# Turning activations by DMA transpositions of 16-bit planes instead of TensorE transpositions, in a transformer stack on one core

## The chip, the core and the metric

The kernel runs on one core of one Trainium2 chip. The metric is the device time of one execution in microseconds (us). TensorE (PE, with its weight loads PEld) multiplies and transposes into PSUM; VectorE (DVE), ScalarE (ACT) and GpSimd (POOL) work on SBUF, the first two on PSUM as well; SyncE (SP) issues all DMAs here. Every engine works through its own queue in order and waits for others by semaphores.

## The reference, cut to what matters

The input has 8 sequences of 1024 rows of 256 numbers, all in 32-bit floats. Four blocks follow one another, each with a residual around it:

```
x = x + decoder_layer(layernorm(x))     # linear attention with 16 heads and cumulative sums along the
                                        #   rows, then x @ Wo, layernorm, gelu MLP 256-1024-256, layernorm
x = x + relu(layernorm(x) @ w1 + b1) @ w2 + b2                 # MLP 256-1024-256
x = x + softmax(q k^T / 16) v,   q, k, v from layernorm(x)     # attention over the 1024 rows
x = x + fp4(silu(g) * u) @ fp4(w_down)^T                       # g, u = fp4(layernorm(x)) @ fp4(w_gate / w_up)^T
```

fp4() rounds each 16 numbers of a row to a 4-bit grid with their own scale. Every product contracts over the columns of its left operand, so rows of activations must be turned (columns onto the partitions) before TensorE can take them.

## The kernel before

A chunk is 128 rows, a group 4 chunks; a sequence has two groups, and there are 16 groups. The parts of the program are Python generators: linear attention by groups (`linear_group`, `linear_span`, `linear_chunk`), the two MLPs (`dense`, with `norms_1` and `norms_2` after each), and softmax attention with the fp4 MLP by chunks (`soft_chunk`). A generator yields what it needs next: the engine, the tiles that must be ready, PSUM banks or a fresh buffer, and a due time `at`. The class `Plan` keeps an estimated clock of every engine and of every tile, takes the part whose need is met first on TensorE's clock, and writes its instructions down; each engine's order is then fixed by dependencies (`Queue.issue`). Where the plan foresees TensorE pausing for more than 1.6 us, `fill` puts in dummy products of the identity for the pause less 0.7 us. Nearly all instructions are recorded at one line, L342.

Buffers of each kind come from fixed sets (`TILES`); late in the kernel `SPARE` lets prob tiles lie in flow's buffers, soft in lin's, rows in x's, and the tiles of q and k serve as two more `hid`. The weights of the MLPs are streamed through four buffers each (`w_in`, `w_out`): their loads wait on SP until TensorE has used the buffer.

Rows are turned in two ways:

- `turned` transposes 128x128 pieces on TensorE against the identity into a PSUM bank, and ACT (or DVE, for every second probT) copies the bank to SBUF. It serves n0T (two pieces a chunk), k (two), probT (eight), xqT (two) and hqT (six).
- `flip` serves h, n and n2T, three pairs of pieces a chunk. POOL copies the 32-bit rows into two planes of 16-bit halves (`cut`), SP issues one DMA transposition of the four 128x128 planes (`spun`), and ACT interleaves the halves again into the target.

Of the kernel before, what the change touches and what calls it, by code (L numbers as in the profile page):

```python
# [9 lines left out]
F32 = mybir.dt.float32  # L10
I32 = mybir.dt.int32
BF16 = mybir.dt.bfloat16
U16 = mybir.dt.uint16
# [4 lines left out]
P = 128  # L18
# [26 lines left out]
    "x": (4, D, F32),  # L45
    "n0": (2, D, F32),
    "lin": (4, D, F32),
    "flow": (9, 512, F32),
    "xr": (2, D, F32),
    "norm": (3, D, F32),  # L50
    "hidden": (LAG + 2, D, F32),
    "soft": (5, D, F32),
    "prob": (7, 512, F32),
    "rows": (4, D, F32),
    "hid": (3, INTER_PAD, F32),
    "q_c": (2, INTER, BF16),
    "cut": (2, 2 * D, U16),
    "spun": (2, 2 * D, U16),
}


# [4 lines left out]
class Plan:  # L66
# [96 lines left out]
    def took(self, queue, op, args, kw):  # L163

        aps = [x for x in list(args) + list(kw.values()) if isinstance(x, bass.AP)]
        outs = [kw["out"] if "out" in kw else aps[0]]
        if kw.get("accum_out") is not None:
            outs.append(kw["accum_out"])
        size = 1
        for ap in aps:  # L170
            n = 1
            for d in ap.shape[1:]:
                n *= d
            size = max(size, n)

        overlap, after = 0.0, 0.035
        if queue == "tensor":
            size = 1
            for d in outs[0].shape[1:]:
                size *= d  # L180
            cost = size * (0.853e-3 if op == "transpose" else 1.687e-3)
            tiled = op == "matmul" and (kw["lhsT"].shape[-1] <= 32 or kw["lhsT"].shape[0] <= 32)
            if tiled or op == "matmul" and kw["lhsT"].dtype == BF16:
                cost *= 0.25
            if tiled != self.tiled:
                cost += 0.2
            self.tiled = tiled
            after = 0.2
        elif queue == "vector":
            each = {"reciprocal": 6.2e-3, "tensor_tensor_scan": 2.15e-3}.get(op, 1.05e-3)  # L190
            cost = 0.17 + each * size
            if op == "tensor_scalar" and outs[0].dtype == BF16:
                cost = 0.16 + 0.26e-3 * size
            elif op == "scalar_tensor_tensor" and any(ap.shape[-1] == 1 for ap in aps):
                cost += 0.06
            overlap = 0.08
        elif queue == "scalar":
            cost = (0.16 if op == "copy" else 0.26) + 0.82e-3 * size
            for x in args:
                if not isinstance(x, bass.AP) and self.SETS.get(x, self.act_set) != self.act_set:  # L200
                    self.act_set = self.SETS[x]
                    self.free[queue] = self.free.get(queue, 0.0) + 1.3
            if kw.get("accum_out") is not None:
                cost += 0.15
            overlap = 0.1
        elif queue == "gpsimd":
            cost = 0.65 + 0.7e-3 * size
            if op in ("tensor_scalar", "iota"):
                cost = 0.22
            elif op == "memset":  # L210
                cost = 0.1 + 0.9e-3 * size
            elif op == "tensor_copy":
                cost = 0.15 + 1.0e-3 * size
        else:
            cost = 0.4
        start = self.free.get(queue, 0.0)
        if queue not in ("tensor", "sync"):
            start = max([start] + [self.used.get(ap.tensor.name, 0.0) for ap in outs])
        for ap in aps:
            name = ap.tensor.name  # L220
            if self.by.get(name) != queue or queue in ("vector", "gpsimd"):
                start = max(start, self.done.get(name, 0.0) + (0.05 if queue == "gpsimd" else 0.0))
            if name not in self.done and name in self.held:
                start = max(start, self.used[name])
        if queue == "tensor":
            if start - self.ran > 2.0:
                self.slow = start + 2.1
            if start < self.slow:
                cost *= 2
            self.ran = start + cost  # L230
        if queue == "sync":
            start = max(start, self.landed.pop(0))
        end = start + cost
        if queue == "sync":
            n = 2e-6 / 150e-3 if op == "dma_start_transpose" else 4e-6 / 250e-3
            for d in outs[0].shape:
                n *= d
            self.free["rings"] = max(self.free.get("rings", 0.0), end) + n
            after = self.free["rings"] - end + 2.1
            self.landed.append(end + after)  # L240
        self.free[queue] = end - overlap
        for ap in outs:
            self.done[ap.tensor.name] = end + after
            self.by[ap.tensor.name] = queue
        for ap in aps:
            name = ap.tensor.name
            self.used[name] = max(self.used.get(name, 0.0), end + after)
            if queue != "tensor" and name not in self.kept:
                self.held.discard(name)
# [111 lines left out]
def block_stack_kernel(ctx: ExitStack, tc: tile.TileContext, a: dict, out: bass.AP):  # L361
# [272 lines left out]
            nc.tensor.transpose(bank[:, i, :], src, ident)  # L634
        return bank[:, : len(srcs), :]

    def flip(src, dst):

        cut = yield from fresh("cut", plan.pool(src))
        nc.gpsimd.tensor_copy(  # L640
            cut.rearrange("p (h f) -> p h f", h=2),
            src.bitcast(U16).rearrange("p (f h) -> p h f", h=2),
        )
        plan.drop(src)
        spun = yield from fresh("spun", dma(cut))
        nc.sync.dma_start_transpose(out=spun.rearrange("p (b t) -> p b t", t=P), in_=cut)
        plan.drop(cut)
        yield act(spun)
        nc.scalar.copy(
            dst.bitcast(U16).rearrange("p k (t h) -> p k t h", h=2),  # L650
            spun.rearrange("p (h k t) -> p k t h", h=2, t=P),
        )
        plan.drop(spun)

    def table(func):

# [265 lines left out]
    def turn_half(p, kind, i, src):  # L922
        dst = half_of(p, kind, i // 2)
        j = i % 2
        yield from flip(src, dst[:, :, j * P : (j + 1) * P])
        n = groups[p]["turned"]
        n[kind, i // 2] = n.get((kind, i // 2), 0) + 1

    def linear_group(p):
# [9 lines left out]
        def front(i):  # L939
# [4 lines left out]
            rc = groups[p]["res"][i] = kept([P, D], "res", RES)  # L944
            n0 = yield from layernorm("n0", x)
            plan.drop(x)
            yield pe(n0, banks=1)
            bank = turned(halves(n0))
            yield act(bank)
            nc.scalar.copy(n0T[:, :, i * P : (i + 1) * P], bank)  # L950
            fronts.add(i)
            yield plan.need("gpsimd", (n0, bo), when=lambda: "norm" in late)
            nc.gpsimd.tensor_tensor(rc, n0, bo, ALU.add)
# [193 lines left out]
    def linear_chunk(p, i, n0T, comp, qk):  # L1147
# [86 lines left out]
            scores.append(sc)  # L1234
        end = g == NG - 1 and i == G - 1
        if not end:
            yield pe(banks=1, at=at + 0.66 + 0.06 * i, when=lambda: count["attended"] == c)
            bank = turned([qk[1][:, k, here] for k in range(2)])
            kT = two((yield from fresh("lin", act(bank), "k")))
            nc.scalar.copy(kT, bank)  # L1240
        kv = past.get("kv")
        yield pe(
            pad,
# [237 lines left out]
    def norms_2(p, i, acc, taken):  # L1481
# [15 lines left out]
            q["n2T"][g] = two(kept([P, 2 * GT], "n2T", 4))  # L1497
        n2 = q["n2T"][g]
        here = slice(i * P, (i + 1) * P)
        yield from flip(n, n2[:, :, here])  # L1500
        yield pe(
            n2,
            banks=1,
# [14 lines left out]
    def soft_chunk(cc):  # L1518
# [49 lines left out]
            plan.let_go(banks[kb])  # L1568
        rows = yield from fresh("rows", dma())
        nc.sync.dma_start(out=rows, in_=q["rows", c])  # L1570
        probT = []
        for kb in range(NG):
            yield pe(prob[kb], banks=1, at=at + 0.25)
            bank = turned([prob[kb][:, j * P : (j + 1) * P] for j in range(G)])
            plan.drop(prob[kb])
            tp = yield from fresh("prob", act(bank) if kb % 2 else dve(bank), "probT")
            tp = tp.rearrange("p (k t) -> p k t", k=G)
            (nc.scalar.copy if kb % 2 else nc.vector.tensor_copy)(tp, bank)
            probT.append(tp)
        yield pe(*probT, banks=1)  # L1580
        rsum = small([P, 1], "rsum")
        nc.vector.tensor_reduce(rsum, sums, AX.X, ALU.add)
        nc.vector.reciprocal(rsum, rsum)
# [14 lines left out]
        n = yield from layernorm("soft", rows)  # L1598
        yield dve(n)
        yield from fp4(n, D)  # L1600
        yield pe(n, banks=1, at=at + 0.5, when=lambda: "fp4" in weights)
        bank = turned(halves(n))
        plan.drop(n)
        xqT = two((yield from fresh("soft", act(bank), "xqT")))
        nc.scalar.copy(xqT, bank)
        hid = None
        for j0 in range(0, INTER, INTER // 2):
            cols = slice(j0, j0 + INTER // 2)
            yield pe(xqT, banks=2)
            gb, ub = mm_bank()[:, : INTER // 2], mm_bank()[:, : INTER // 2]  # L1610
            for bank, wT in ((gb, wgT), (ub, wuT)):
                for k in range(2):
# [14 lines left out]
        plan.drop(xqT)  # L1627
        yield dve(hid)
        yield from fp4(hid, INTER)
        hqT = []  # L1630
        for half in range(2):
            yield pe(hid, banks=1, at=at + 0.75)
            tiles = INTER_TILES[4 * half : 4 * half + 4]
            bank = turned([hid[:, f0 : f0 + P] for f0, _ in tiles])
            hqT.append((yield from fresh("prob", act(bank), "hqT")))
            hqT[half] = hqT[half].rearrange("p (k t) -> p k t", k=4)
            nc.scalar.copy(hqT[half][:, : len(tiles), :], bank)
        yield pe(*hqT, banks=1)
        bank = mm_bank()
        for k in range(len(INTER_TILES)):  # L1640
            nc.tensor.matmul(
# [3 lines left out]
                start=k == 0,  # L1645
                stop=k == len(INTER_TILES) - 1,
            )
        plan.drop(hid, *hqT)
        count["out"] += 1
        y = yield from fresh("soft", dve(bank), "y")  # L1650
        nc.vector.tensor_tensor(y, bank[:, :D], rows, ALU.add)
# [68 lines left out]
```

## Time and profile before

| | before |
|---|---|
| three runs, us | 2618.31, 2614.11, 2616.58 (median 2616.58) |
| profiled execution, us | 2618.8, span 2617.1 |
| granted TensorE clock | 0.997 |
| TensorE busy in the span | 98% |
| VectorE, ScalarE, GpSimd busy | 74%, 51%, 27% |
| DMA queue 1, share of 16 engines | 33.1% |
| DMA transpositions | 192 |

Times in rows of the profile are microseconds, means of one instruction nanoseconds. A group's row has the engine, the operation, the tiles written and read by the program's names, the shapes and the count; then the busy time, the mean of one, and the engine's idle time just before with what ended it. Spans of matmuls overlap since they are pipelined: their steps from start to start are read from the timeline. A product of 32-bit floats appears as two records, a transposition as one. L342 is the helper that records every instruction, so groups are told apart by tiles.

### The profile page before, as it was taken

How to read it: one execution, taken by the hardware profiler on the slowest of the kernel's cores; microseconds unless marked ns; L12 is line 12 of the kernel's file. 1: busy time of each engine (PE TensorE's matmuls, PEld its weight loads, DVE VectorE, ACT ScalarE, POOL GpSimd, SP SyncE). 2: the span in 40 equal slices, each digit the busy share in tenths (PEclk: the TensorE clock that was granted, in tenths of full speed). 3: DMA queues.
4: the chain of work that ended last, by engine and by line, in shares of the span. 5: the costliest groups of instructions: out<-in, count | busy, mean ns of one | idle time of the engine just before them, and what ended most of it. 6: DMA issues, size and time to landing. Idle time of an engine off the chain costs nothing.

```text
span 2617.1 us, 46326 instructions
## 1 busy us (share of the span) xinstructions
PE 2571.5 (98%) x16593; PEld 2010.4 (77%) x16593; DVE 1947.3 (74%) x4352; ACT 1344.0 (51%) x2658; POOL 703.0 (27%) x1293
## 2 busy tenths in 40 slices
PE   8998999999999999999999999999999999999999
PEld 7777777877777777777877877777777777878777
DVE  6788796867769587685868768677785877855687
ACT  3535636464475544645555464645545545454443
POOL 2343332332313232131321322313231231311000
PEclk9999999999999999999999999999999999999999
DMA  2445443333323342322433323333333423333100
GB/s 75 125 121 154 115 117 95 109 88 107 86 80 101 85 115 68 108 80 85 117 81 92 97 75 99 92 108 81 99 82 83 115 72 96 88 87 89 31 5 21
DMA packets 391268, 237.11 MB, mean 91 GB/s; under 512 B 129152, under 2 KB 379520, under 8 KB 391040
## 3 DMA queue, kind: packets, MB, share of 16 engines
q1 hardware_dynamic: 391040, 234.16, 33.1%
q8 instruction: 132, 2.16, 0.4%
q14 instruction: 96, 0.79, 0.1%
HBM read 188.17 MB, written 20.71 MB: 80 GB/s over the span
## 4 chain that ended last, share of the span: by engine, by line
PE 80%; DVE 13%; ACT 3%; DMA 1%; issue 1%; POOL 1%; SPq 0%; DVEq 0%; POOLq 0%; ACTq 0%
PE bank L342 80%; DVE hid L342 2%; DVE prod L342 2%; DVE n L342 1%; ACT L342 1%; DVE ln_st L342 1%; DVE u L342 1%; DVE res L342 1%; DVE ln_mv L342 0%; DVE x_amax L342 0%; DMA spread<-packed 0%; DVE div L342 0%; DVE spread L342 0%; DVE mx L342 0%; DMA spun<-cut 0%
## 5 line engine op out<-in xcount | busy, mean ns | idle before, releaser
L342 PE MATMUL bank<-half,w_in 128*128 128x256 f32 x2048 | 533.4, 384 | 7.3 <-DVE v L342 4.5
L342 PE MATMUL bank<-w_out,hidden 128*128 128x256 f32 x2048 | 529.4, 383 | 2.7 <-DMA w_out<-in_L_ffn_w_dram 1.6
L342 POOL TENSOR_SCALAR ln_ve<-ln_mv 128x1 f32<-128x1 f32 x384 | 96.9, 252 | 1607.8 <-DVE ln_mv L342 1591.3
L342 PEld LDWEIGHTS bank<-w_out,hidden 128*128 128x128 f32 x2048 | 374.0, 190 | 105.2 <-issue 53.2
L342 PEld LDWEIGHTS bank<-half,w_in 128*128 128x128 f32 x2048 | 384.3, 191 | 85.6 <-issue 22.5
L342 ACT ACT_TABLE_LOAD x321 | 411.8, 1283 | 17.3 <-DVE nmax L342 11.6
L342 ACT ACTIVATE hidden<-bank,c_L_ffn_b 128x256 f32<-128x256 f32 x256 | 120.6, 472 | 269.4 <-PE bank L342 269.1
L342 POOL TENSOR_TENSOR ln_rstd<-ln_ve,neghalf 128x1 f32<-128x1 f32 x384 | 236.3, 615 | 32.0
L342 PE MATMUL bank<-n2T,qT 128*128 128x512 f32 x512 | 241.6, 594 | 0.4 <-ACT qT L342 0.2
L342 PE MATMUL bank<-vt,probT 128*128 128x256 f32 x1024 | 232.0, 380 | 0.0
L342 PEld LDWEIGHTS bank<-vt,probT 128*128 128x128 f32 x1024 | 193.1, 190 | 30.2 <-issue 3.0
L342 ACT ACTIVATE hidden<-bank,c_L_attn_b 128x256 f32<-128x256 f32 x256 | 119.7, 468 | 183.3 <-PE bank L342 182.8
L342 PE MATMUL bank<-wdT,hqT 128*128 128x256 f32 x768 | 176.6, 380 | 1.2 <-ACT hqT L342 1.0
L342 PE MATMUL bank<-wgT,xqT 128*128 128x352 f32 x512 | 173.8, 462 | 0.0
L342 PE MATMUL bank<-wuT,xqT 128*128 128x352 f32 x512 | 172.4, 459 | 0.0
L342 ACT COPY half<-spun 128x512 uint16<-128x512 uint16 x128 | 86.3, 674 | 150.1 <-DMA spun<-cut 149.6
L342 PEld LDWEIGHTS bank<-wdT,hqT 128*128 128x128 f32 x768 | 145.3, 190 | 22.7 <-ACT hqT L342 1.4
L342 DVE TENSOR_TENSOR sc<-bank,triu 128x512 f32<-128x512 f32 x240 | 149.7, 680 | 8.5 <-PE bank L342 8.0
L342 PEld LDWEIGHTS bank<-n2T,qT 128*128 128x128 f32 x512 | 93.4, 190 | 69.1 <-issue 60.5
L342 PEld LDWEIGHTS bank<-wuT,xqT 128*128 128x128 f32 x512 | 97.4, 190 | 54.1
L342 DVE TENSOR_TENSOR hid<-hid,bank 128x352 f32<-128x352 f32 x116 | 59.7, 515 | 101.4 <-PE bank L342 79.2
L342 PEld LDWEIGHTS bank<-wgT,xqT 128*128 128x128 f32 x512 | 93.7, 190 | 37.1 <-issue 4.3
(220 smaller groups left out, 4530.2 us busy)
## 6 DMA issues: line engine op xcount, KB each, us to landing
w_in<-in_L_attn_W_dram SPq DMA_DIRECT2D x256, 128.0 KB
w_out<-in_L_attn_W_dram SPq DMA_DIRECT2D x256, 128.0 KB
w_in<-in_L_ffn_w_dram SPq DMA_DIRECT2D x256, 128.0 KB
w_out<-in_L_ffn_w_dram SPq DMA_DIRECT2D x256, 128.0 KB
spread<-packed SPq DMA_DIRECT2D x90, 256.0 KB
x<-in_L_attn_inputs_dram SPq DMA_DIRECT2D x64, 128.0 KB
xr<-in_L_attn_inputs_dram SPq DMA_DIRECT2D x64, 128.0 KB
rows<-res SPq DMA_DIRECT2D x64, 128.0 KB
```

Of the source, the lines that this page charges most:

```text
L342: ins = method(*args, **kw)
```

## The change

All rows that `turned` served are now turned by `flip`, except in the first group (`near`), where `flip` itself uses TensorE, for h as well. `flip` takes a pair of 128x128 pieces; `flip_all` starts several at once, and counts the pairs cut and done. The tiles for probT and hqT are taken before their sources are dropped. Cut and spun get four buffers each, prob loses one and flow one. The plan's estimates for a transposition's issue and landing, and for the copies around it, are changed. Weights ("fp4", "softmax") are still turned by TensorE.

```diff
-    "flow": (9, 512, F32),
+    "flow": (8, 512, F32),
-    "prob": (7, 512, F32),
+    "prob": (6, 512, F32),
-    "cut": (2, 2 * D, U16),
-    "spun": (2, 2 * D, U16),
+    "cut": (4, 2 * D, U16),
+    "spun": (4, 2 * D, U16),
...
-            cost = 0.4
+            cost = 1.2 if op == "dma_start_transpose" else 0.4
...
-            after = self.free["rings"] - end + 2.1
+            after = self.free["rings"] - end + (0.6 if op == "dma_start_transpose" else 2.1)
...
-    def flip(src, dst):
-
+    def flip(src, dst, tiles=None, last=None, near=False):
+
+        if near:
+            yield pe(src, banks=1)
+            bank = turned([src[:, k, :] for k in range(2)])
+            if last is not None:
+                plan.drop(last)
+            yield act(bank)
+            nc.scalar.copy(dst, bank)
+            return
         cut = yield from fresh("cut", plan.pool(src))
         nc.gpsimd.tensor_copy(
-            cut.rearrange("p (h f) -> p h f", h=2),
-            src.bitcast(U16).rearrange("p (f h) -> p h f", h=2),
-        )
-        plan.drop(src)
+            cut.rearrange("p (h k t) -> p h k t", h=2, k=2),
+            src.bitcast(U16).rearrange("p k (t h) -> p h k t", h=2),
+        )
+        if last is not None:
+            plan.drop(last)
+        if tiles is not None:
+            tiles.cut += 1
         spun = yield from fresh("spun", dma(cut))
         nc.sync.dma_start_transpose(out=spun.rearrange("p (b t) -> p b t", t=P), in_=cut)
         plan.drop(cut)
         yield act(spun)
         nc.scalar.copy(
             dst.bitcast(U16).rearrange("p k (t h) -> p k t h", h=2),
-            spun.rearrange("p (h k t) -> p k t h", h=2, t=P),
+            spun.rearrange("p (h k t) -> p k t h", h=2, k=2),
         )
         plan.drop(spun)
+        if tiles is not None:
+            tiles.done += 1
+
+    def flip_all(pairs, at):
+
+        tiles = SimpleNamespace(cut=0, done=0)
+        for src, dst in pairs:
+            plan.start(flip(src, dst, tiles), at)
+        return tiles
...
-            yield pe(n0, banks=1)
-            bank = turned(halves(n0))
-            yield act(bank)
-            nc.scalar.copy(n0T[:, :, i * P : (i + 1) * P], bank)
+            yield from flip(two(n0), n0T[:, :, i * P : (i + 1) * P], near=p == 0)
...
-            yield pe(banks=1, at=at + 0.66 + 0.06 * i, when=lambda: count["attended"] == c)
-            bank = turned([qk[1][:, k, here] for k in range(2)])
-            kT = two((yield from fresh("lin", act(bank), "k")))
-            nc.scalar.copy(kT, bank)
+            k_at = at + 0.66 + 0.06 * i
+            need = plan.pool(at=k_at, when=lambda: count["attended"] >= c - (p > 0))
+            kT = two((yield from fresh("lin", need, "k")))
+            yield from flip(qk[1][:, :, here], kT, near=p == 0)
...
-        probT = []
+        probT, flips = [], []
         for kb in range(NG):
-            yield pe(prob[kb], banks=1, at=at + 0.25)
-            bank = turned([prob[kb][:, j * P : (j + 1) * P] for j in range(G)])
+            tp = yield from fresh("prob", plan.pool(prob[kb], at=at + 0.25), "probT")
+            probT.append(tp.rearrange("p (k t) -> p k t", k=G))
+            rows_kb = prob[kb].rearrange("p (k t) -> p k t", k=G)
+            flips.append(
+                flip_all([(rows_kb[:, j : j + 2], probT[kb][:, j : j + 2]) for j in (0, 2)], at + 0.25)
+            )
+        for kb in range(NG):
+            yield plan.pool(when=lambda: flips[kb].cut == 2)
             plan.drop(prob[kb])
-            tp = yield from fresh("prob", act(bank) if kb % 2 else dve(bank), "probT")
-            tp = tp.rearrange("p (k t) -> p k t", k=G)
-            (nc.scalar.copy if kb % 2 else nc.vector.tensor_copy)(tp, bank)
-            probT.append(tp)
-        yield pe(*probT, banks=1)
+        yield pe(*probT, banks=1, when=lambda: all(f.done == 2 for f in flips))
...
-        bank = turned(halves(n))
-        plan.drop(n)
-        xqT = two((yield from fresh("soft", act(bank), "xqT")))
-        nc.scalar.copy(xqT, bank)
+        xqT = two((yield from fresh("soft", plan.pool(n, at=at + 0.5), "xqT")))
+        yield from flip(two(n), xqT, last=n)
...
-            bank = turned([hid[:, f0 : f0 + P] for f0, _ in tiles])
-            hqT.append((yield from fresh("prob", act(bank), "hqT")))
...
+        for j in range(0, len(INTER_TILES), 2):
+            src = two(hid[:, j * P : (j + 2) * P])
+            pairs.append((src, hqT[j // 4][:, j % 4 : j % 4 + 2]))
+        flips_h = flip_all(pairs, at + 0.75)
...
+        yield pe(*hqT, banks=1, when=lambda: flips_h.done == len(pairs))
```

More of the change, by code (lines that the diff above doesn't have):

```diff
@@ L197, in took @@
         elif queue == "scalar":
-            cost = (0.16 if op == "copy" else 0.26) + 0.82e-3 * size
+            cost = (0.16 if op == "copy" and outs[0].dtype != U16 else 0.26) + 0.82e-3 * size
             for x in args:
@@ L212, in took @@
             elif op == "tensor_copy":
-                cost = 0.15 + 1.0e-3 * size
+                cost = 0.2 + 1.0e-3 * size
         else:
-            cost = 0.4
+            cost = 1.2 if op == "dma_start_transpose" else 0.4
         start = self.free.get(queue, 0.0)
@@ L924, in turn_half @@
         j = i % 2
-        yield from flip(src, dst[:, :, j * P : (j + 1) * P])
+        yield from flip(two(src), dst[:, :, j * P : (j + 1) * P], last=src, near=p == 0)
         n = groups[p]["turned"]
@@ L1499, in norms_2 @@
         here = slice(i * P, (i + 1) * P)
-        yield from flip(n, n2[:, :, here])
+        yield from flip(two(n), n2[:, :, here], last=n)
         yield pe(
@@ L1600, in soft_chunk @@
         yield from fp4(n, D)
-        yield pe(n, banks=1, at=at + 0.5, when=lambda: "fp4" in weights)
-        bank = turned(halves(n))
-        plan.drop(n)
-        xqT = two((yield from fresh("soft", act(bank), "xqT")))
-        nc.scalar.copy(xqT, bank)
+        xqT = two((yield from fresh("soft", plan.pool(n, at=at + 0.5), "xqT")))
+        yield from flip(two(n), xqT, last=n)
         hid = None
@@ L1608, in soft_chunk @@
             cols = slice(j0, j0 + INTER // 2)
-            yield pe(xqT, banks=2)
+            yield pe(xqT, banks=2, when=lambda: "fp4" in weights)
             gb, ub = mm_bank()[:, : INTER // 2], mm_bank()[:, : INTER // 2]
@@ L1629, in soft_chunk @@
         yield from fp4(hid, INTER)
-        hqT = []
+        hqT, pairs = [], []
         for half in range(2):
-            yield pe(hid, banks=1, at=at + 0.75)
-            tiles = INTER_TILES[4 * half : 4 * half + 4]
-            bank = turned([hid[:, f0 : f0 + P] for f0, _ in tiles])
-            hqT.append((yield from fresh("prob", act(bank), "hqT")))
-            hqT[half] = hqT[half].rearrange("p (k t) -> p k t", k=4)
-            nc.scalar.copy(hqT[half][:, : len(tiles), :], bank)
-        yield pe(*hqT, banks=1)
+            tq = yield from fresh("prob", plan.pool(hid, at=at + 0.75), "hqT")
+            hqT.append(tq.rearrange("p (k t) -> p k t", k=4))
+        for j in range(0, len(INTER_TILES), 2):
+            src = two(hid[:, j * P : (j + 2) * P])
+            pairs.append((src, hqT[j // 4][:, j % 4 : j % 4 + 2]))
+        flips_h = flip_all(pairs, at + 0.75)
+        yield plan.pool(when=lambda: flips_h.cut == len(pairs))
+        plan.drop(hid)
+        yield pe(*hqT, banks=1, when=lambda: flips_h.done == len(pairs))
         bank = mm_bank()
@@ L1647, in soft_chunk @@
             )
-        plan.drop(hid, *hqT)
+        plan.drop(*hqT)
         count["out"] += 1
```

## The prediction

> **What bounds the kernel now.** I read the busy times first, then the shares of the chain that ended last, both on the page.
>
> ```profile
> PE 2571.5 (98%) x16593; PEld 2010.4 (77%) x16593; DVE 1947.3 (74%) x4352; ACT 1344.0 (51%) x2658; POOL 703.0 (27%) x1293
> ...
> PE 80%; DVE 13%; ACT 3%; DMA 1%; issue 1%; POOL 1%; SPq 0%; DVEq 0%; POOLq 0%; ACTq 0%
> ```
>
> TensorE (PE) is busy for 98% of the span and holds 80% of the chain. A busy PE need not be a full one, so next come the stretches and the PE's own waits:
>
> ```profile
> 1300.00:1800.00 500.00, 495.64 (x3329) 386.03 (x3328) 371.79 (x835) 269.21 (x523) 135.18 (x259) 1.00 0.34 90
> ```
> ```profile
> PE bank L342 <- DVE kv L342: 4.8, 3, 1.9
> ```
>
> The stretch shows PE 495.64 of 500 us busy at full granted clock, the DMA engines at 0.34; the second line is PE's largest wait on anything, 4.8 us in all. So PE work is the time, and instructions taken from PE come off it one for one unless new waits appear. The groups kept apart by shape, and the timeline of PE, show what a transposition costs:
>
> ```profile
> L342 PE MATMUL bank<-ident,prob 128*128 128x128 f32 x464 | 70.4, 274 | 3.0 <-ACT prob L342 1.9 <-DVE res L342 0.4
> L342 PE MATMUL bank<-ident,hid 128*128 128x128 f32 x348 | 56.2, 273 | 1.1 <-DVE hid L342 1.0
> L342 PE MATMUL bank<-ident,n 128*128 128x128 f32 x256 | 46.9, 274 | 2.0 <-DVE sc L342 1.4 <-DVE n L342 0.7
> ```
> ```profile
> 1208.80 0.60 PE L342 MATMUL bank<-ident,prob 128*128 128x128 f32 x4
> 1209.23 1.06 PE L342 MATMUL bank<-n0T,wk 128*128 128x512 f32 x2
> ```
>
> The mean of 274 ns is latency and overlaps the next; in the timeline four take 1209.23 - 1208.80 = 0.43 us, 0.109 us each. That is the price I use.
>
> The DMA way is already there for h, n and n2T (192 flips). Its tile view says what one costs and who waits:
>
> ```profile
> L342 SPq DMA_TRANSPOSE spun<-cut x192: 1188/1197/2336, 56.4 to 2437.6; - x192
> L342 ACT COPY half<-spun x128: 656/675/694, 59.6 to 2387.5; 128x512 uint16<-128x512 uint16 x128
> ...
>   DMA spun<-cut: 170.0, 94
> ...
>   PEld bank L342: 10.0, 9
>   PE bank L342: 5.2, 4
> ```
>
> SP is held 1.197 us per issue, ACT copies for 0.675 us and idles 170 us in all, 0.885 us per flip, at the head of its queue; of that PE feels 5.2 us (its weight loads 10.0).
>
> **What the Trainium skill says.** "TensorE: Matmul & The Clock Gate", Part 4, puts a transposition in a kernel at about 275 ns; the rows agree (274), but the step between pipelined ones is 0.109. "VectorE: DVE Perf Modes", The three transpose paths, gives 390 ns for TensorE and 1309 ns for the DMA crossbar: slower alone, so only freed PE time can pay for it. "DMA: Bandwidth & Descriptors", Issuing engines are not separate DMA queues: every queue shares 16 DMA engines; here there is one queue, at 33.1%. "SBUF — State Buffer", SBUF: two separate sides: GpSimd and VectorE take an exclusive lock on a shared port pair. The trace agrees: the clean cut takes 0.61 us, and this one, beside a DVE scan, 1.54:
>
> ```profile
> 1889.50 1.54 POOL L342 COPY cut<-n 128x512 uint16<-128x512 uint16 x1
> ...
> 1891.43 1.19 SPq L342 DMA_TRANSPOSE spun<-cut  x1
> ...
> 1895.52 0.68 ACT L342 COPY half<-spun 128x512 uint16<-128x512 uint16 x1 [3.88 <-DMA spun<-cut]
> ```
>
> ACT sat 3.88 us behind that flip, and PE ran on: 4 us of lateness is covered in mid-kernel.
>
> **The change, part by part.** The order of instructions of both programs gives the counts.
>
> *Removed from PE:* the transpositions of prob and its spare buffers 464 + 48 = 512, of hid and its two spares 348 + 36 = 384, of n 240 and of k 104, less 8 of h that are added for the first group: 1232. The flips give the same: 808 after, 192 before, each in place of two. So 1232 x 0.109 = **-134.3 us** on the bound. Removing it needs no cover.
>
> *Added to PE:* the program writes dummy ident matmuls where it foresees PE pauses over 1.6 us. They go from 137 to 220 instructions, 83 x 0.22 us (274 records for 137, 0.11 each) = **+18.4 us**. They stand in 17 places, not 9; each leaves about 0.7 us unfilled: 8 x 0.7 = **+5.6**. Three of the new places (52 instructions, 11 us) are at the very end, where before a chunk's last transposition and copy took 1.4 us (2609.60 to 2610.98) and now three flips take 0.61 + 3 x 1.197 + 1.2 to land + 0.675 = 6.1 us with nothing else left. The other five are in mid-kernel.
>
> *ACT:* +616 copies x 0.674 = 415 us, less the copies out of PSUM: n0T 60, k 52, xqT 64 and hqT 64 at 0.373, hqT 64 at 0.585, probT 64 at 0.592 = 165; +8 small ones, 3. Net +253, to 1597 of some 2530 us (63%): beside PE, costed at nothing as long as its waits stay covered. *DVE:* -64 probT copies, 43 us. *POOL:* +616 x 0.61 = 376 us, to 1079 (43%), hidden by its idle time, except for the lock: a DVE norm that meets a cut grows from about 0.40 to 0.66, so up to 0.255 x 616 = 157 us of DVE, for 81% at most. *SP:* 808 x 1.197 + some 1530 other issues at 0.38 = 1550 us (61%). *DMA engines:* a flip fills them 0.92 us at most (three 1-us stretches around the flip at 56.4: 0.08 + 0.25 + 0.59), so 866 + 616 x 0.92 = 1433 us, 57%. None of these is the bound by its sum.
>
> *Latency:* a flip of one pair takes 0.61 + 1.2 + 1.2 + 0.67 = 3.7 us from cut to copied, where TensorE took about 0.8; probT (four flips) 7.3. What covers it is the PE work that the order puts between producer and consumer: laying the matmuls' steps end to end, the median from a chunk's last score to its first vt matmul goes from 27 to 24 us (shortest 8 to 11), from vt to the gate 26 to 25, from the up matmul to wdT 24 to 27 (shortest 6.5 to 12). So it is covered nearly everywhere. If not, PE stops at vt, gate or wdT.
>
> *Buffers:* prob 7 to 6, flow 9 to 8, cut and spun 2 to 4. Prob tiles are held longer (probT is taken before prob is dropped); the price is in the order, as the fills. k's turn may start a chunk earlier.
>
> *What the order does not show:* lateness of flips in the real queues, where a flip stands on SP behind a weight load that waits for PE:
>
> ```profile
> SPq L342 <- PE bank L342: 1115.1, 785, 10.3
> ```
>
> and ACT's head-of-line waits. From below: the 192 flips cost PE 5.2 us, 0.027 each, so 17 us for 616. From above: 15.2 with the weight loads, 0.079, so 49. I take 0.045, **+28 us**. No gain is likely here, since PE has no other waits to lose.
>
> *Sum* on the profiled execution, 2618.8 us (span 2617.1): 2618.8 - 134.3 + 18.4 + 5.6 + 28 = 2536.5. The median of the three runs is 2.2 lower: **2534 us**.
>
> **Rivals.** (1) *Late flips are felt in part.* SP is 61% full with a queue that stops at each weight load (785 waits, mean 1.4 us), and cuts meet DVE. At 0.11 us per added flip: 2618.8 - 134.3 + 24 + 68 - 2.2 = 2574. For it: 4.2 times as many flips on the queues; against it: PE's small waits now. (2) *Slower: ACT's in-order waits become the pace.* At 0.885 us per added flip ACT idles 545 us more, on 253 us more work; then `hidden` and `sc` come late and PE stops at w_out. The gain is gone once more than (134 - 24) / 616 = 0.18 us of each flip's wait is seen by PE; at 0.3 it is 2618.8 - 134.3 + 24 + 185 - 2.2 = 2691. Against it: PE felt 0.027 of 0.885. (3) *The flips hide wholly:* 2618.8 - 134.3 + 24 - 2.2 = 2506. That the transpositions stay on PE is excluded by the counts.
>
> **How the numbers follow.** My forecast (2534, with rival 3 as its lower end) 0.62, rival 1 0.26, near no change 0.03, rival 2 0.09. Range 2500 to 2600: from all hidden with a few us of fewer pauses, to 0.15 us felt per flip. About 0.2% (5 us) is what a measurement of this kernel can tell from no change. Faster 0.88, same 0.03, slower 0.09.
>
> **What would show it.** Right: PE busy near 2455 to 2480, the ident rows of prob, hid and k gone, waits of PE on copied flips under 50 us, ACT near 1600 us, a last wdT 5 us after hid. Wrong: PE under 94% in mid-kernel with waits on ACT hidden, probT or hqT in sum over 110 us, or DVE stretched over 90%.

## The result, and the profile after

The changed kernel takes 2655.1 us (median of four runs, 2649.2 to 2658.4) against 2615.8 for the kernel before beside it: 1.0147 times, 95% interval 1.0126 to 1.0168. It is 1.5% slower; the forecast was 3% faster.

The page of the changed kernel, busy times and then the chain that ended last:

```profile
PE 2502.3 (94%) x15527; PEld 1907.7 (72%) x15527; DVE 1986.2 (75%) x4288; ACT 1560.2 (59%) x2900; POOL 1129.5 (43%) x1909
...
PE 32%; DVE 30%; ACT 13%; DMA 10%; issue 7%; POOL 7%; SPq 2%; POOLq 0%; DVEq 0%; ACTq 0%
```

PE has lost work, as it should (2571.5 to 2502.3 us busy), but its idle time grew from 2617.1 - 2571.5 = 45.6 to 2651.6 - 2502.3 = 149.3 us, and the chain runs through every engine instead of along PE. No other engine is near full. The stretch that was shown of before:

```profile
1300.00:1800.00 500.00, 480.41 (x2948) 365.48 (x2948) 391.76 (x834) 309.95 (x571) 227.09 (x386) 1.00 0.54 128
```

PE is idle 19.6 us of these 500 where it was 4.4. What PE waits for (us in all, times, longest):

```profile
PE bank L342 <- ACT xqT L342: 22.3, 16, 3.1
PE bank L342 <- POOL kv_sum L342: 16.9, 9, 5.3
PE bank L342 <- ACT qT L342: 16.8, 14, 2.8
PE bank L342 <- ACT half L342: 14.1, 11, 3.9
...
PE bank L342 <- ACT probT L342: 0.6, 3, 0.2
```

It hardly waits for the new probT. xqT and `half` are copies of flips themselves, xqT of a new one and `half` of one that was there before. qT is no flip at all: ACT brings it in between the copies of flips. kv_sum is a sum of POOL's. The tile view of the flips:

```profile
L342 SPq DMA_TRANSPOSE spun<-cut x808: 1188/1191/2802, 81.6 to 2644.0; - x162
...
  DMA spun<-cut: 526.6, 404
...
  POOL cut L342: 165.5, 103
...
  PEld bank L342: 86.2, 79
  PE bank L342: 49.6, 48
```

ACT idles 526.6 us for flips, in 404 of 808; before it was 170 us in 94 of 192. PE itself waits 49.6 us for copies of flips, where it was 5.2, and about as much again, 38.6 us, for five tiles of ACT's that are no flips (qT, e, xo, qz, hidden). POOL, too, now waits, for cut buffers that a transposition still holds. And why flips are late is seen in SP's own queue, SP, POOL and ACT in one stretch of the timeline:

```profile
1322.32 1.35 POOL L342 COPY cut<-n 128x512 uint16<-128x512 uint16 x2
...
1322.76 0.53 SPq L342 DMA_DIRECT2D w_in<-in_L_ffn_w_dram  x1
1323.40 1.19 SPq L342 DMA_TRANSPOSE spun<-cut  x1
1324.68 0.53 SPq L342 DMA_DIRECT2D w_out<-in_L_ffn_w_dram  x1
1325.32 1.19 SPq L342 DMA_TRANSPOSE spun<-cut  x1
...
1326.03 0.68 ACT L342 COPY half<-spun 128x512 uint16<-128x512 uint16 x1 [1.43 <-DMA spun<-cut]
1326.76 0.70 PE L342 MATMUL bank<-half,w_in 128*128 128x256 f32 x2 [0.68 <-ACT half L342]
```

Two cuts end by 1323.67; SP issues a weight load, one flip, another load, the next flip, each in turn and almost without a pause; the copy of `half` comes when the first of them has landed, 2.6 us after its issue, and PE stops 0.68 us for it. Pairing the n-th cut with the n-th transposition (both queues are in order), a flip waits 2.47 us on the mean from the end of its cut to its issue, where it was 0.35 us before. Added up from the trace, SP spends 1.16 of the 2.47 us issuing other flips and 0.76 issuing plain DMAs, and stands still for 0.55. So it is SP's own issuing that makes flips late, more than loads that stand waiting for PE; SP's waits on PE were longer before, 1115.1 us:

```profile
SPq L342 <- PE bank L342: 467.2, 487, 30.1
```

The transfers themselves are not slower: the copies that waited for their flip start 3.00 us after its issue began on the mean, and 2.96 before.

### The profile page after: what moved, and what is told of

Read it like the earlier page. It is cut to its first block, busy times and chain, and to the rows that moved or that the text cites. A ratio compares the mean times of both kernels' runs of the same rounds, so it can differ in the third digit from the quotient of the medians.

```text
span 2651.6 us, 46663 instructions
## 1 busy us (share of the span) xinstructions
PE 2502.3 (94%) x15527; PEld 1907.7 (72%) x15527; DVE 1986.2 (75%) x4288; ACT 1560.2 (59%) x2900; POOL 1129.5 (43%) x1909
## 3 DMA queue, kind: packets, MB, share of 16 engines
q1 hardware_dynamic: 726144, 314.98, 49.1%
## 4 chain that ended last, share of the span: by engine, by line
PE 32%; DVE 30%; ACT 13%; DMA 10%; issue 7%; POOL 7%; SPq 2%; POOLq 0%; DVEq 0%; ACTq 0%
PE bank L342 32%; DMA spun<-cut 9%; ACT L342 5%; DVE hid L342 4%; DVE n L342 4%; DVE ln_st L342 3%; DVE prod L342 2%; DVE u L342 2%; POOL cut L342 2%; POOL ln_rstd L342 2%; DVE sc L342 2%; SPq L342 2%; DVE res L342 1%; DVE x_amax L342 1%; DVE ln_mv L342 1%
## 5 line engine op out<-in xcount | busy, mean ns | idle before, releaser
L342 PE MATMUL bank<-half,w_in 128*128 128x256 f32 x2048 | 534.6, 384 | 18.0 <-ACT half L342 14.1
L342 PEld LDWEIGHTS bank<-w_out,hidden 128*128 128x128 f32 x2048 | 380.3, 192 | 120.6 <-issue 55.6
L342 PE MATMUL bank<-n2T,qT 128*128 128x512 f32 x512 | 246.2, 605 | 17.3 <-ACT qT L342 16.8
L342 POOL COPY cut<-n 128x512 uint16<-128x512 uint16 x248 | 183.6, 746 | 134.9 <-DVE n L342 75.5
L342 ACT COPY probT<-spun 128x512 uint16<-128x512 uint16 x256 | 168.5, 674 | 122.6 <-DMA spun<-cut 121.9
L342 POOL COPY cut<-prob 128x512 uint16<-128x512 uint16 x226 | 160.1, 726 | 179.0 <-DMA spun<-cut 96.3
L342 PE MATMUL bank<-wgT,xqT 128*128 128x352 f32 x512 | 177.6, 470 | 23.5 <-ACT xqT L342 22.3
L342 ACT COPY hqT<-spun 128x512 uint16<-128x512 uint16 x192 | 127.1, 676 | 95.6 <-DMA spun<-cut 95.0
L342 POOL COPY cut<-hid 128x512 uint16<-128x512 uint16 x174 | 117.6, 699 | 143.0 <-DVE hid L342 112.5
```

Of the source, the lines that this page charges most:

```text
L342: ins = method(*args, **kw)
```

## The experiments

Two theories at first: **A**, flips come late and stop ACT at the head of its queue, and PE pays for what ACT then brings late; **B**, POOL is the trouble (616 more cuts, the port shared with DVE). A third, **C**, is that ACT's added copies are too much. Times are medians of four or more runs beside the kernel before; the ratio is to that. Runs 1, 2, 3, 5 and 6 leave out a part of the work, as said at each.

**1. No wait for flips at ACT.** Same order of instructions (in the diffs dst16, src16 and pos16 stand for the rearranged 16-bit views).

```diff
-        nc.scalar.copy(dst16, spun)     # reckoned and placed as before, but
+        nc.scalar.copy(dst16, pos16)    # reads the constant tile pos as 16-bit planes
```

> The order of instructions is that of the changed kernel; cut copies on POOL and DMA transpositions on SP are all issued, but ACT's 808 copies read a constant tile of the same shape in place of spun (the turned values are left out), so ACT never waits for a flip. Theory A (late flips stop ACT at the head of its queue, and PE waits for what ACT then brings late): PE's waits on ACT tiles go, 2520 to 2550 us. Theory B (POOL is the trouble: 616 more cuts, the shared port and the waits for cut buffers delay norms and kv sums): stays at 2620 to 2650. Theory C (ACT's 253 us of added work is simply too much): stays at 2630 to 2655.

Measured: 2548.2 us, ratio 0.9734 (0.9719 to 0.9748). Its busy times:

```profile
PE 2469.0 (97%) x15527; PEld 1900.7 (75%) x15527; DVE 1988.4 (78%) x4288; ACT 1535.3 (60%) x2900; POOL 1132.7 (44%) x1909
```

107 us go with the waits alone, while ACT, DVE and POOL do the work of the changed kernel. Flips are still issued late (2.42 us after the cut), but nobody waits for them. PE's waits fall on copies of flips (xqT from 22.3 to 7.7 us, `half` from 14.1 to 1.1) and on qT, which is none (16.8 to 5.7). Theory A holds, C falls, and B as the main cause too. The run frees both kinds of tiles at once, so it does not say how much of the 107 us belongs to each.

**2. No transpositions either.** The `dma_start_transpose` is only reckoned, not issued.

> As the last, and the 808 DMA transpositions are left out too (SP and the DMA engines do not see them; cuts are made and read by nobody). If SP's issue time of 1.19 us each and the DMA traffic hurt beyond the flips' own lateness (weight loads late, cut buffers freed late), this is 10 us or more below the last run: 2500 to 2530. If only lateness at ACT counts, the two agree within 5 us. Theory B: 2600 to 2640. Theory C: 2630 to 2650.

Measured: 2544.8 us, 0.9721 (0.9707 to 0.9736). 3.4 us below the last: SP's issue time and the DMA traffic of 808 flips cost next to nothing except through the flips' own lateness.

**3. Small cuts.** Same order.

```diff
-            cut.rearrange("p (h k t) -> p h k t", h=2, k=2), src16
+            cut[:, 0:1], src16[:, 0, 0:1]
```

> Same order as the changed kernel; POOL's cut writes one column instead of 512 (the rest of the planes is left out and holds zeros), so a cut takes about 0.1 us instead of 0.61 and hardly holds the shared port; DMA transpositions and ACT's waits for them stay. Theory B: 2540 to 2580. Theory A: flips come 0.5 us earlier, and POOL has 570 us less to do, so a part: 2590 to 2640. Theory C: 2640 to 2655.

Measured: 2605.1 us, 0.9956 (0.9940 to 0.9973), 50 us below the changed kernel. ACT still idles 511.3 us for flips; PE's waits for kv_sum fall from 16.9 to 11.2 us, DVE's busy time from 1986 to 1896. So POOL's part is real but the smaller one, and as ACT's waits hardly fall, most of it is not on the way of the flips but beside it. The parts overlap: 107 and 50 are together more than the 149 us between the changed kernel and the forecast's 2506 with flips wholly hidden.

**4. The landing reckoned as before.** One line of the change undone.

```diff
-            after = self.free["rings"] - end + (0.6 if op == "dma_start_transpose" else 2.1)
+            after = self.free["rings"] - end + 2.1
```

> One line of the change undone: the plan again reckons 2.1 us from issue to landing of a transposition in place of 0.6, so that the order puts 1.5 us more other work ahead of each ACT copy. Theory A: ACT's waits on flips fall from 527 us to under 250, time 2570 to 2620 us. Theories B and C: no gain, 2645 to 2665.

Measured: 2634.4 us, 1.0062 (1.0047 to 1.0077). 21 us gained, less than A's 35 to 85, and the waits of ACT fell to 322.8 us, not under 250. The new estimate leaves the order too little cover, but that is a fifth of the 107 us of run 1. Part of what more cover gains is given back, because the plan then foresees more pauses of PE. The dummy products of the changed kernel and of this run:

```profile
L342 PE MATMUL bank<-ident 128*128 128x128 f32 x440 | 54.6, 283 | 3.1 <-POOL ident masks.py:199 3.1
L342 PE MATMUL bank<-ident 128*128 128x128 f32 x684 | 82.5, 279 | 3.1 <-POOL ident masks.py:199 3.1
```

The 244 records more are 27 us at the prediction's 0.11 us each, an estimate. The issue is still reckoned at 1.2 us in place of 0.4, so this is 0.8 us more cover than in the kernel before.

**5. No weight loads after the first four buffers of each.** Same order on all engines but SP.

```diff
+                        if n >= W_FF:
+                            w = ws[n - W_FF]   # reckoned as loaded, nothing issued
```

> Same order on PE, ACT, POOL and DVE as the changed kernel; of the streamed MLP weights only the first four of w_in and of w_out are loaded, and stay (1016 loads left out, products use old weights). SP then has no load that waits for PE ahead of a flip, and 1016 fewer issues of 0.4 us. Theory A1 (flips are late because they stand on SP behind weight loads and each other): ACT's waits on flips fall by more than half, 2560 to 2600 us. Theory A2 (late because cuts are late, and because 2.4 us from issue to copy is more than the order leaves): 2630 to 2655.

Measured: 2587.0 us, 0.9882 (0.9865 to 0.9899). 68 us gained, within A1's range: flips are late because they stand on SP behind loads and behind each other. From cut to issue 1.54 us instead of 2.47, ACT's waits 371.5 instead of 526.6. Of the 1.54 us SP issues other flips for 0.83 and plain DMAs for 0.17, and stands still for 0.55 as in the changed kernel: what the loads cost the flips was their issuing, not their waits for PE. PE's own waits for loads, 3.5 us, go as well. (A1's "by more than half" was too much.)

**6. Both 3 and 5.**

> The changed kernel's order with both earlier cuts into the lateness at once: cuts of one column (the other columns left out) and only the first four of each weight buffer loaded. Small cuts alone gave 50 us, loads left out 68. If they act on separate parts of a flip's way (POOL and SP) they add up to what the removal of ACT's waits gave, 107 us: 2540 to 2560 us. If both free the same wait: 2575 to 2590.

Measured: 2524.0 us, 0.9643 (0.9628 to 0.9657), 131 us below the changed kernel and below both ranges: 50 and 68 add up, and a little more. The page and the tile view of this run:

```profile
PE 2461.6 (98%) x15527; PEld 1900.7 (75%) x15527; DVE 1898.6 (75%) x4288; ACT 1554.2 (62%) x2900; POOL 768.2 (30%) x1913
```
```profile
  DMA spun<-cut: 284.5, 249
...
  PE bank L355: 17.5, 15
```

All 808 flips are issued, landed, waited for and copied here; ACT still idles 284.5 us for them, and PE is 98% busy. The DMA transpositions and ACT's copies fit beside PE; what did not fit was their lateness, with POOL's time for full cuts, which this run leaves out too.

**7 to 9. Parts of the change alone.** First only n0T, k and xqT by DMA, then only prob and hid, then the latter with the landing of run 4. The diff is of run 8; run 7 instead has the lines of the kernel before for prob and hid.

```diff
-            yield from flip(qk[1][:, :, here], kT, near=p == 0)
+            yield from flip(qk[1][:, :, here], kT, near=True)   # run 8, n0T alike, xqT by its old lines
```

> Only n0T, k and xqT are turned by DMA (176 flips more than before, less 8); prob and hid go back to TensorE. Theory U (every added flip costs the same, 148 us of lost PE time over 616 flips, 0.24 us against 0.22 gained): 2615 to 2625 us. Theory V (flips with little work between producer and consumer, k, n0T and xqT, carry the loss): 2625 to 2640.

Measured: 2611.0 us, 0.9974 (0.9966 to 0.9981), 6.6 us gained for some 37 us taken off PE (168 flips, 336 x 0.109): 30 us lost, 0.18 per flip, a little less than either theory had it.

> Only prob and hid are turned by DMA (448 flips more, 896 transpositions or 98 us off PE); n0T, k and xqT go back to TensorE. Theory U: 2620 to 2635 us. Theory V: the long covers hold, 2560 to 2595.

Measured: 2626.5 us, 1.0033 (1.0022 to 1.0045), 8.8 us lost in spite of 98 us off PE: 107 us, 0.24 per flip, as theory U has it. Theory V was mine and is wrong: prob and hid have 24 to 27 us of other work between producer and consumer, and lose more than the small ones. PE waits only 17.5 us for copies of flips here. A likely reason, which no run tests by itself, is that prob and hid come in bursts of four and three, and ACT, at the head of its queue, holds up what has nothing to do with them.

> As the last, with the landing reckoned at 2.1 us as before. Fewer waits of ACT on flips: 10 to 25 us below the last run by theory A, as the same line gave 21 us with all flips; the same as the last if its covers are long enough already.

Measured: 2598.8 us, 0.9926 (0.9912 to 0.9941), 27.7 us below, a little more than expected. ACT's waits fall from 423 to 156.9 us.

**10 to 13. Loads that do not stand waiting.**

```diff
-        times += [self.used.get(x.tensor.name, 0.0) for x in need.unused]
+        times += [self.used.get(x.tensor.name, 0.0) + (2.0 if need.queue == "sync" else 0.0) for x in need.unused]
```

> The changed kernel; the plan lets a weight load go to SP only 2 us after the time at which it reckons the buffer unused, so that a load seldom stands waiting for PE ahead of a flip. Theory A1 (SP's queue, stopped by loads that wait for PE, makes flips late, and each lateness makes PE and so the next load later): SP's wait on PE falls from 467 us to under 250, cut end to issue from 2.5 us to about 1.5, time 2585 to 2625, as leaving the loads out gave 2587. If it is SP's sheer issue time: 2640 to 2660.

Measured: 2639.6 us, 1.0085 (1.0068 to 1.0102). 15.5 us gained, little, and at the edge of what was expected if SP's sheer issue time is the reason. SP's wait on PE did fall (467.2 to 314.8), but cut to issue stayed at 2.43. Of that SP issues for 1.80, much as in the changed kernel (1.92). This speaks against A1's loads that stand waiting.

> As the last, with the landing reckoned at 2.1 us as in the kernel before. If the two remedies act on different parts of the lateness they add: 2560 to 2605 us. If both only put off the same waits: within 10 us of the better one.

Measured: 2632.2 us, 1.0056 (1.0041 to 1.0071). Not added: within 3 us of the landing alone. With all 808 flips neither remedy is enough.

> Only prob and hid by DMA, landing 2.1 us, loads 2 us later. By A1 below the 2599 us of the version without late loads: 2565 to 2590. If SP, with 24% fewer flips, is no longer what makes them late: 2590 to 2605.

Measured: 2573.9 us, 0.9831 (0.9817 to 0.9846), **the fastest version that leaves nothing out, 1.7% below the kernel before.** The time is in A1's range, but the 25 us below run 9 do not come by A1's way: ACT's waits on flips are no shorter (177.2 us against 156.9), and from cut to issue it is 1.89 us against 2.04. What gives them is not shown. Its flips, 632:

```profile
  DMA spun<-cut: 177.2, 137
...
  PEld bank L342: 29.2, 42
  PE bank L342: 12.5, 11
```

> Only prob by DMA (256 flips more, 512 transpositions or 56 us off PE), landing 2.1 us, loads 2 us later. If few flips are nearly free: 2565 to 2580 us (56 us less about 10). If the loss grows with the number of flips alone, this is the best of all; if not, the last run is.

Measured: 2617.4 us, 1.0003 (0.9992 to 1.0013). A miss: 56 us off PE, nothing gained. PE's first wait there is ACT e, 18.5 us in 11; how the plan came to this order was not followed.

**14 to 17. What was still open.** The change without its flips, the kernel before with late loads, hid alone, and hid with the small ones.

> The change without its flips: n0T, k, xqT, prob and hid by TensorE as before, but the new estimates, one prob and one flow buffer fewer, four cut and spun, h of the first group by TensorE. If the whole loss lies in the added flips: within 5 us of before, 2612 to 2622. If the rest of the change costs something that no flip explains: 2625 to 2645.

Measured: 2619.9 us, 1.0010 (1.0001 to 1.0019). Buffers, estimates and the first group cost 2.7 us by themselves; the loss lies in the added flips.

> The kernel before with its weight loads 2 us later, no other change. If late loads only help flips to come in time, 192 of which are seldom late: 2612 to 2622 us. If they are a gain by themselves: 2590 to 2608, and the 25 us that they gave with prob and hid by DMA say little of flips.

Measured: 2611.7 us, 0.9980 (0.9971 to 0.9988). Late loads are worth 5.6 us without any new flip, so of the 25 us that they gave in 12 (2598.8 to 2573.9) some 6 may be their own.

> Only hid by DMA (192 flips more, 384 transpositions or 42 us off PE), landing 2.1 us, loads 2 us later. Prob alone gave nothing, prob with hid 43 us: if hid's flips are the free ones, 2570 to 2585 us, level with both together; if the gain needs both, 2600 to 2618.

Measured: 2601.2 us, 0.9935 (0.9917 to 0.9953), between the two expectations: 16 us for 42 off PE.

> hid, n0T, k and xqT by DMA, prob by TensorE, landing 2.1 us, loads 2 us later (368 flips more, 736 transpositions or 80 us off PE). If the number of flips and bursts decides (632 flips were well covered, 808 not): 2560 to 2590 us. If n0T, k and xqT, which stand ahead of other work on ACT, are what costs: 2595 to 2625.

Measured: 2614.1 us, 0.9987 (0.9977 to 0.9997), 3 us for 80 off PE: k, n0T and xqT add a loss here, though alone (run 7) they gained 6.6 us. Prob alone gains nothing, hid alone 16, both 43. Each version is planned afresh, so its covers differ; why the sum is more than its parts stays open.

**18. More cover for the fastest version.**

> The best version (prob and hid by DMA, loads 2 us later) with the landing reckoned at 3.0 us in place of 2.1. If ACT's remaining 177 us of waits on flips still cost: 2560 to 2570. If the longer covers cost more dummy products and held buffers than they save: 2574 to 2595.

Measured: 2583.7 us, 0.9875 (0.9854 to 0.9895). ACT's waits halve (177.2 to 89.3), but PE gains nothing from it: of the three landings that were tried with prob and hid, 2.1 us is the best.

## Why the prediction was wrong, by its own steps

- **What bounds the kernel, and what is taken off it: right.** The transpositions left PE as counted, and so did the dummy products come in; run 6, with much of the lateness and the full cuts out, shows PE 98% busy at 2524 us. The forecast's sum with flips wholly hidden was 2506.
- **ACT, DVE, POOL and SP by their sums: nearly right.** ACT 1560 us (forecast 1597), POOL 1130 (1079), DVE 1986 at 75% (up to 81%), the DMA queue 49.1% (57 at most). SP's issues, added up from the trace, take 1739 us, not 1550: 66%, since one takes 1.25 us on the mean for a flip and 0.475 for another DMA, not the 1.197 and 0.38 of the sum. None is full, as forecast. But "costed at nothing as long as its waits stay covered" was the whole question, and the covers were judged by the PE work between a flip's producer and its own consumer. For probT that work is there: PE waits 0.6 us on it in all. It did not cover xqT, whose 25 us before the gate were reckoned too, and where PE waits 22.3 us. For `half`, n0T and k no cover was reckoned. Nor was one for what stands behind the flips in ACT's queue, as qT. The sign that was to show the forecast right, waits of PE on copied flips under 50 us, came out at 49.6 with the gain gone: it counts only a part of what late flips cost.
- **The step that failed is "late flips, 0.045 us each, +28 us".** The price was carried over from 192 flips to 808 as if lateness grew with their number alone. It is 2655.1 - 2506 = 149 us, 0.24 us for each added flip, above the upper bound of 0.079 and above the 0.218 us (two transpositions) that a flip saves. What failed is the price's own premise: before, a flip was issued 0.35 us after its cut; with 4.2 times as many on SP it is 2.47, of which SP issues other flips and loads for 1.92. Rival 1 named SP's queue, at 0.11 us per flip: half the size. It gave the queue's fullness and its stops at weight loads as reasons; the stops became shorter (467.2 us of waits on PE, 1115.1 before), and the queue's own issuing is what grew. The one flip that was shown as covered, 3.88 us late with PE running on, was taken for the rule; in the changed kernel PE waits for `half` 11 times, 14.1 us in all.
- **Rival 2 (slower) named the price and the point:** more than 0.18 us per flip felt by PE, through ACT's in-order waits. It came true at 0.24, and run 1 takes out 107 of the 149 us by freeing ACT alone. The other 42 us are not taken apart; run 3 and run 6 point to the full cuts. Where it said that PE would stop, at w_out, PE hardly does (6.6 us in all before these products): it stops at the gate, at the scores and at w_in. Its chance of 0.09 was too low. Its counterargument, that PE felt only 0.027 us of 0.885, was the extrapolation that failed: ACT's idle time per flip fell from 0.885 to 526.6 / 808 = 0.65 us, and PE felt more of it.
- **The new estimate of the landing** was listed in the change and has no price in the prediction. With it undone the kernel gains 21 us with all flips and 28 with prob and hid. Counted from the start of the issue to the data's being ready, with the plan's 0.87 us for the transfer, the plan reckoned 0.4 + 0.87 + 2.1 = 3.37 us before, reckons 1.2 + 0.87 + 0.6 = 2.67 now, and 4.17 in run 4. Of the 404 copies that waited for their flip, half started within 2.58 us, but 111 took more than 3: the new estimate fits the usual flip and leaves no margin for the late ones.
- **Buffers:** rightly small by themselves (2.7 us for everything but the flips).

## What to carry to other kernels

An operation taken from a full engine and given to a chain of three in-order queues is paid by its own consumer when it is late, and also by what stands behind it in those queues; look at the queue it waits in, at what one issue holds that queue for, and at who is next, before calling it covered. Do not scale a wait per instruction by the count when the count loads the queue that makes the wait. In an order fixed ahead, an estimate of a transfer with a margin can be worth more than one that fits the usual case; here a landing of 2.1 us was better than 0.6, and also better than 3.0. Loads that the same queue issues ahead of such transfers cost them their issue time, with what follows from it 68 us at most here.

## What was not expected of the hardware

After a stop PE can be slow for a while, in this kernel. Four stretches around PE's wait for ACT e in the changed kernel (stretch, its length, then PE, PEld, DVE, ACT and POOL busy, granted clock, share of the DMA engines, GB/s):

```profile
655.60:657.60 2.00, 0.53 (x3) 0.13 (x1) 1.89 (x7) 1.80 (x6) 1.07 (x3) 1.00 0.33 98
657.60:659.60 2.00, 1.66 (x10) 1.53 (x11) 1.93 (x5) 0.80 (x4) 0.67 (x3) 1.00 0.14 37
659.60:663.00 3.40, 3.40 (x10) 2.68 (x9) 3.26 (x8) 0.66 (x2) 3.40 (x6) 0.50 0.32 90
663.00:667.00 4.00, 4.00 (x21) 3.49 (x20) 3.72 (x12) 2.54 (x6) 0.07 (x1) 1.00 0.61 143
```

A wait of 1.8 us is followed by 3.4 us at half the clock, in which PE counts as fully busy. The trace's record of the granted clock has 15 such stretches at 0.50 in the changed kernel, 54.6 us in all, and four before, 14.2 us. Of the 15, 12 have waits of PE of more than 1 us in sum in the 7 us ahead of them; but of PE's 31 waits over 1.5 us, 18 have no such stretch within 4 us, so a stop alone does not tell. The mean granted clock fell from 0.997 to 0.990, and was 0.997 again in runs 1 and 6. Half of 54.6 - 14.2 is about 20 us: an estimate of the part of the 149 us that is slow clock rather than waiting. It agrees in kind with PE's busy time, 2502.3 us in the changed kernel and 2469.0 in run 1 for the same 15527 instructions. No run held the clock and kept the waits, so this part is read from the profile and not tested. Runs 1 and 6 also work on constants or zeros in place of the turned values; that this helped their clock is not excluded, though run 7, which leaves nothing out, has 0.999.
